# A four-layer graph network: row sums and powers of the first batch chunk by chunk, a corrected model time in the planner, and the last batch's gates with features on partitions

## The chip, the cores and the metric

The kernel runs on one core of one Trainium2 chip. The time is the device time of one execution in microseconds (us). All executions quoted are of the fast state: on one core the state is judged by the time alone, and none was set aside. Each profile is one execution; its span is 1.8 to 2.4 us shorter than the time of the same execution. "Product" below means a matrix product on TensorE.

## The reference, cut

32 graphs of 512 nodes with 128 features go through four layers. Each layer normalizes x per node, takes the positive part h, and adds the layer's output to x. A is `adj`, 512 x 512 per graph.

```python
def reference(x, adj, ...):
    h = relu(layernorm(x)); x = x + L0(h, adj)   # (D^-1/2 (A+I) D^-1/2) h W + b, leaky relu; D = row sums of A+I
    h = relu(layernorm(x)); x = x + L1(h, adj)   # elu of three projections, A and A^T times two of them, tanh
    h = relu(layernorm(x)); x = x + L2(h, adj)   # four sub-layers f1..f4 with A scaled by its row and column norms
    h = relu(layernorm(x)); x = x + L3(h, adj)   # m = tanh(A (h Wm)); r, z, n gates of a GRU; (1-z) n + z h
    return x
```

## The kernel before: the parts that the argument touches

The kernel doesn't issue its instructions as written. It records every operation with a model time, and a list scheduler (`Plan.order`) lays all 32 batches out in that model: a free engine takes, of its ready operations, the one whose due time is earliest. The result is a fixed order on each engine. In these kernels each engine follows that order and waits by semaphores. So a model time costs nothing by itself, but decides what stands in front of what.

```python
class Plan:
    def order(self):
        ...
            due = o.batch * PERIOD if o.batch < B - 1 else (B - 2) * PERIOD + ENDING
            o.key = (due - o.tail + o.later if o.rank is None else o.rank - 1e6, i)
        ...                         # event by event: an idle engine takes the ready operation of least key

    def t_act(n, pointers=0):                  # model time of a ScalarE operation of n columns
        return 0.09 + 0.093 * pointers + n / 1150
    def t_pow(n):                              # model time of a GpSimd power, n wide
        return 0.9 + 0.1 * n
```

The normalization in front of each layer (moments on VectorE, the power -1/2 on GpSimd, `nb` on VectorE, four `h` on ScalarE), the 512 x 128 transposition through DRAM, and `f`:

```python
        def normed(xin, out_tag, extra=None):
            ...                                                  # bn_stats and bn_aggr of 4 chunks -> mv
            # in moments(): v = variance + eps
            op("DVE", 0.08, lambda: nc.vector.tensor_scalar_add(v8.ap()[:, 0:NC], mv.ap()[:, :, 1], LN_EPS), ...)
            op("POOL", t_pow(n), lambda: nc.gpsimd.tensor_tensor(inv..., v8..., neg_half[:, :n], op=ALU.pow), ...)   # sc
            op("DVE", 0.08, ..., [mv, inv], [nb])
            for c in range(NC):
                op("ACT", t_act(D, 2), ..., [xin, nb, inv], [(h, {c})])          # h = relu(x * inv + nb)
        def turned(m, name):
            op("DVE", t_tt(N), lambda: nc.vector.transpose(blk..., m...), [m], [blk])
            for k in range(NC):
                op("SP", 0.4, lambda k=k: away(k), [blk], [(bounce, {k})], kb=64)      # turn_<name>, to DRAM
            op("SP", 0.4, lambda: nc.sync.dma_start(mT.ap(), bounce.tile), [bounce], [mT], kb=256)   # and back
        ...
        # row and column norms of A: to DRAM, spread over all partitions, put in order by ScalarE
        op("SP", 0.4, spread, [bounce], [spaced], kb=512)
        op("ACT", t_act(2 * N), lambda: nc.scalar.copy(rows..., spaced.ap().rearrange("p n k -> p k n")), [spaced], [rows])
        ...
            op("ACT", t_act(N, 1), ..., [ps, CF], [f_new])                             # f1 .. f4 = tanh(ps + b)
        ...
            f4 = turned(f[0], "f4r")                                                   # f4 back to rows
            tt(x3, lambda: nc.vector.tensor_add(x3, x2, turned_cols(f4)), ...)         # xr <- xr,f4r
        h3, _ = normed(x3, "h")
```

Where TensorE's plan has a gap of over 0.7 us, mostly in the first 60 us, filler products (`ps_idle`) are inserted to keep its clock up.

Names used below: `agg` is layer 0's aggregate and `lin` its product with W; `rep` is a projection of layer 1 after elu, `u` that layer's update; `sd` is a product with layer 2's weights plus its bias, which the aggregations with A take.

Of the kernel before, what the change touches and what calls it, by code (L numbers as in the profile page):

```python
# [13 lines left out]
F32 = mybir.dt.float32  # L14
AF = mybir.ActivationFunctionType
ALU = mybir.AluOpType
AX = mybir.AxisListType

P = 128
B, N, D = 32, 512, 128  # L20
NC = N // P
# [3 lines left out]
PERIOD = 30.0  # L25
ENDING = 6.0
SMALL = 16


SEVEN = {"last": 0 * 5 * D, "mid": 1 * 5 * D, "gates": 2 * 5 * D}  # L30
# [9 lines left out]
W_L2 = []  # L40
# [18 lines left out]



C_L1_NODE, C_L2 = 0, 1
C_COLS = C_L2 + 4 * len(L2_CHUNKS)



# [193 lines left out]
def gnn_stack(  # L260
# [21 lines left out]
    rf_sb = const.tile([P, len(L2_CHUNKS) * 2 * D], F32, name="rf_sb")  # L282
    cf_sb = const.tile([P, len(L2_CHUNKS)], F32, name="cf_sb")
    t_sb = const.tile([P, T_COLS], F32, name="t_sb")
    ident = const.tile([P, P], F32, name="ident")
    neg_half = const.tile([P, 2 * NC], F32, name="neg_half")

    def wt(col, n=D):
        return w_sb[:, col:col + n]
# [8 lines left out]
    def t_tt(n, pointers=0):  # L298
        return 0.065 + 0.058 * pointers + n / 960

    def t_ts(n):
        return 0.07 + n / 1920

    def t_act(n, pointers=0):
        return 0.09 + 0.093 * pointers + n / 1150

    def t_pool(n):
        return 0.15 + n / 450

    def t_pow(n):  # L310
        return 0.9 + 0.1 * n

    def op(*args, **kwargs):
        return plan.op(*args, **kwargs)

    def const_buf(name, ap):
        b = Buf(plan, name, name, None)
        b.tile, b.slot = ap, 0
        return b

    W1, W2F, W3, CS, RS, RF, CF, TS, ID, NH = (const_buf(n, t) for n, t in (
        ("w1", w_sb), ("w2", w_sb), ("w3", w_sb), ("c_sb", c_sb), ("r_sb", r_sb), ("rf_sb", rf_sb),
        ("cf_sb", cf_sb), ("t_sb", t_sb), ("ident", ident), ("neg_half", neg_half)))

    def mm(ps, out_of, lhs, rhs, n, start, stop, reads, later=0.0):
        op("PE", t_mm(n), lambda: nc.tensor.matmul(out_of(ps.ap()), lhs(), rhs(), start=start, stop=stop),  # L326
           reads, [ps], later=later)
# [9 lines left out]
    def setup():  # L337
# [1 line left out]

        op("POOL", 1.0, lambda: make_identity(nc, ident), [], [ID])  # L340
        op("POOL", 0.2, lambda: nc.gpsimd.memset(neg_half, -0.5), [], [NH])
        first = W_L2[0][0]

        def spread(lo, hi, to=None):
            return lambda: nc.sync.dma_start(
                r_sb[:, lo:hi] if to is None else to.ap()[:, :hi - lo], bass.AP(tensor=brow.tensor, offset=brow.offset + lo, ap=[[0, P], [1, hi - lo]]))
# [2 lines left out]
        op("AQ", 0.5, lambda: nc.scalar.dma_start(w_sb[:, :D], w[:, :D]), [], [(W1, {0})], kb=64)  # L349
        op("AQ", 0.5, lambda: nc.scalar.dma_start(  # L350
            r_sb[:, :D], bass.AP(tensor=brow.tensor, offset=brow.offset, ap=[[0, P], [1, D]])), [], [(RS, {0})], kb=64)
        op("SP", 0.5, lambda: nc.sync.dma_start(c_sb, bcol), [], [CS], kb=9, rank=2)
        op("SP", 0.5, lambda: nc.sync.dma_start(w_sb[:, D:first], w[:, D:first]), [], [(W1, {1})], kb=(first - D) / 2, rank=5)
        op("SP", 0.5, spread(D, R_L3_MSG), [], [(RS, {1})], kb=(R_L3_MSG - D) / 2, rank=5)
        op("SP", 0.5, spread(R_L3_MSG, R_COLS), [], [(RS, {2})], kb=(R_COLS - R_L3_MSG) / 2)
        hrz = plan.buf("s2", (P, N), "hrz")
        op("SP", 0.5, spread(R_L3_HRZ, R_L3_HRZ + 2 * D, hrz), [], [hrz], kb=D)
        op("DVE", 0.4, lambda: nc.vector.tensor_add(r_sb[:, R_L3_G:R_L3_G + 2 * D], r_sb[:, R_L3_G:R_L3_G + 2 * D], hrz.ap()[:, :2 * D]),
           [(RS, {2}), hrz], [(RS, {2})])
        raws = []  # L360
        for i in (0, 2, 3):
            lo, hi = RAW_L2[i][0], RAW_L2[i + 1][0] if i == 2 else RAW_COLS if i == 3 else RAW_L2[2][0]
            buf = plan.buf("s8", (P, NC, N), f"raw{i}")
            op("SP", 0.5, lambda buf=buf, lo=lo, hi=hi: nc.sync.dma_start(
                buf.ap().rearrange("p c n -> p (c n)")[:, :hi - lo], raw[:, lo:hi]), [], [buf], kb=(hi - lo) / 2, rank=3 if i == 0 else 6)
            raws += [(buf, lo)] * (2 if i == 0 else 1)
        op("SP", 0.5, lambda: nc.sync.dma_start(w_sb[:, W_L3_MSG:], w[:, first:]), [], [W3], kb=(W_COLS - W_L3_MSG) / 2)

        def block(i, col):
            buf, lo = raws[i]  # L370
# [48 lines left out]
    def program(b):  # L419
        plan.batch = b  # L420

        def buf(tag, shape=(P, N), name=None):
            return plan.buf(tag, shape, name)
# [3 lines left out]

        rows_shape = (P, NC, D)


        xt, a, aT = buf("s2", rows_shape, "x"), buf("s8", (P, NC, N), "a"), buf("s8", (P, NC, N), "aT")

        pieces = NC if b == 0 else 2

        def load(dst, src, kb, rank):

            n = NC // pieces
            for k in range(pieces):
                s = slice(k * n, (k + 1) * n)
                op("SP", 0.4, lambda s=s: nc.sync.dma_start(dst.ap()[:, s, :], src[:, s, :]),  # L440
                   [], [(dst, set(range(NC)[s]))], kb=kb / pieces, rank=None if b else rank)

        op("SP", 0.4, lambda: nc.sync.dma_start(xt.ap(), x[b]), [], [xt], kb=256, rank=None if b else 0)
        load(a, adj[b], 1024, 1)
        load(aT, adjt[b], 1024, 4)

        def moments(xin, v8):
            st, mv = buf("bn", (P, NC, nc.vector.BN_STATS_DIM)), buf("mv", (P, NC, nc.vector.BN_AGGR_DIM))
            for c in range(NC):
                op("DVE", 0.193, lambda c=c: nc.vector.bn_stats(st.ap()[:, c, :], xin.ap()[:, c, :]), [xin], [(st, {c})])  # L450
            for c in range(NC):
                op("DVE", 0.066, lambda c=c: nc.vector.bn_aggr(mv.ap()[:, c, :], st.ap()[:, c, :]), [(st, {c})], [(mv, {c})])
            op("DVE", 0.08, lambda: nc.vector.tensor_scalar_add(v8.ap()[:, 0:NC], mv.ap()[:, :, 1], LN_EPS), [mv], [(v8, {0})])  # L453
            return mv

        def normed(xin, out_tag, extra=None):


            v8 = buf("v8", (P, 2 * NC))
            n = NC  # L460
            mv = moments(xin, v8)
            if extra:
                extra(v8)
                n = 2 * NC
            inv = buf("sc", (P, 3 * NC))
            op("POOL", t_pow(n), lambda: nc.gpsimd.tensor_tensor(inv.ap()[:, :n], v8.ap()[:, :n], neg_half[:, :n], op=ALU.pow),  # L466
               [v8, NH], [(inv, {0})])
            at = 0
            if extra:
                at = 2 * NC  # L470
                op("DVE", 0.08, lambda: nc.vector.tensor_mul(inv.ap()[:, at:at + NC], inv.ap()[:, 0:NC], inv.ap()[:, NC:2 * NC]),
                   [(inv, {0})], [(inv, {1})])
            nb = buf("nb", (P, NC))
            op("DVE", 0.08, lambda: nc.vector.scalar_tensor_tensor(nb.ap(), mv.ap()[:, :, 0], -1.0, inv.ap()[:, at:at + NC],  # L474
                                                                   op0=ALU.mult, op1=ALU.mult), [mv, inv], [nb])
            h = buf("s2", rows_shape, out_tag)
            for c in range(NC):
                op("ACT", t_act(D, 2), lambda c=c: nc.scalar.activation(  # L478
                    h.ap()[:, c, :], xin.ap()[:, c, :], AF.Relu, bias=nb.ap()[:, c:c + 1],
                    scale=inv.ap()[:, at + c:at + c + 1]), [xin, nb, inv], [(h, {c})])  # L480
            return h, inv
# [157 lines left out]
                    sq.ap(), a.ap()[:, c, :], AF.Copy, accum_out=stat.ap()[:, c:c + 1]), [(a, {c})], [sq, (stat, {c})])  # L639
            op("DVE", 0.08, lambda: nc.vector.tensor_scalar_add(v8.ap()[:, NC:], stat.ap(), 1.0), [stat], [(v8, {1})])  # L640

        hr, inv0 = normed(xt, "h", degree)

        diag = buf("s2", rows_shape, "diag")

        def own(k, n):
            t = aT.ap()
            blocks = bass.AP(tensor=t.tensor, offset=t.offset + k * (N + P), ap=[list(t.ap[0]), [N + P, n], [1, P]])
            nc.gpsimd.tensor_tensor(diag.ap()[:, k:k + n, :], blocks, ident[:, None, :].to_broadcast([P, n, P]), op=ALU.add)

        n = NC if b else 1
        for k in range(0, NC, n):
            op("POOL", t_pool(n * P), lambda k=k, n=n: own(k, n), [(aT, set(range(k, k + n))), ID], [(diag, set(range(k, k + n)))])
        psh = plan.bank("agg")
        for c in range(NC):
            for lo, hi in ((0, c * P), (c * P, (c + 1) * P), ((c + 1) * P, N)):
# [71 lines left out]
        def spread():  # L728
            d = bounce.tile
            nc.sync.dma_start(spaced.ap().rearrange("p n k -> p (n k)"),  # L730
                              bass.AP(tensor=d.tensor, offset=d.offset, ap=[[0, P], [1, 2 * N]]))
# [50 lines left out]
        else:  # L782
# [10 lines left out]
        msg = buf("s2", rows_shape, "msg")  # L793
        tt(msg, lambda: nc.vector.tensor_add(msg.ap(), psm.ap().rearrange("p (c v) -> p c v", c=NC), along(r_sb, R_L3_MSG, D, NC)),
           N, [psm, (RS, {2})])
        psa = plan.bank("agg")
        aT2 = buf("s8", (P, NC, N), "aT2")
        load(aT2, adjt[b], 1024, None)
        aggregate(psa, msg, 0, aT2)
        mT = buf("s2", name="mT")  # L800
        op("ACT", t_act(N), lambda: nc.scalar.activation(mT.ap(), psa.ap(), AF.Tanh), [psa], [mT])

        g = buf("s8", (P, NC, 4 * D), "g")
# [110 lines left out]
```

## Time and profile before

| | before |
|---|---|
| median of 5 runs beside the changed kernel | 2319.75 us (2319.23 to 2321.92) |
| TensorE busy 1000 to 1500 us | 500.00 of 500 us |
| first layer-2 product (`ps_sd<-w_sb,f`) | 57.69 us |
| start of the last aggregation to the end of the span | 2301.6 to 2319.2: 17.6 us |
| TensorE's waits on `f` in the whole run | 3.8 us in 5 waits |

The 57.69 us is of an execution whose head cooled: after a wait of 2.10 us the granted clock was 0.50 from 38 to 40 us and 0.68 in the next 2 us. In the profiles of experiments 4, 6, 7 and 10, in which TensorE's order in the head is the same, the clock stayed at 1.00 there and the same product came at 55.1 to 55.7 us. So a difference of 2 us in this mark between two profiles can be one cold stretch, and the prediction took its base from a cold one.

The prediction below shows the busy table, stretches and waits. One more piece of the kernel before is needed as the yardstick: one pass of the chain that ends in f2, the second `f` of a batch's layer 2. It is the timeline from 1202 to 1210 us. Columns: start, duration (us), engine, line, operation, output<-inputs, sizes, count, and in brackets the idle time of the engine just before with what ended it.

```profile
1202.43 2.07 ACT L735 COPY rows<-spaced 128x1024 f32<-128x1024 f32 x1 [5.91 <-DMA spaced<-bounce]
1203.07 0.69 DVE L784 TENSOR_TENSOR xr<-xr,f4r 128x512 f32<-128x512 f32 x1 [0.21 <-DMA f4r<-turn_f4r]
...
1205.72 0.16 DVE L453 TENSOR_SCALAR v<-mv 128x4 f32<-128x4 f32 x1
...
1205.96 1.11 POOL L466 TENSOR_TENSOR sc<-v,neg_half 128x4 f32<-128x4 f32 x1 [2.57 <-DVE v L453]
1206.12 0.70 DVE L487 STREAM_TRANSPOSE blk<-h 128x512 f32<-128x512 f32 x1
...
1207.10 0.16 DVE L474 SCALAR_TENSOR_TENSOR nb<-mv,sc 128x4 f32<-128x4 f32 x1 [0.28 <-POOL sc L466]
1207.30 1.65 ACT L478 ACTIVATE h<-xr,nb,sc 128x128 f32<-128x128 f32 x4 [1.25 <-DVE nb L474]
1208.85 0.67 ACT L768 ACTIVATE f<-ps_agg,cf_sb 128x512 f32<-128x512 f32 x1
...
1209.77 0.59 PE L326 MATMUL ps_agg<-f,w_sb 128*128 128x512 f32 x1
```

Three batches meet here. `f4r`, `v`, `sc`, `nb` and `h` are layer 3 of batch b-1; `f` and the product are f2 of batch b; `rows` and `blk` are of batch b+1, whose layer-1 `h` is being transposed. On ScalarE f2 stands behind four `h`, so f2 hangs on `xr`, and `xr` on the transfer of `f4r`. The `v` stands **ahead** of `blk`. From the start of the `xr` add to the product it takes 6.7 us, and the product doesn't wait: there is no bracket on it.

### The profile page before, as it was taken

What the parts mean: (1) busy time and instruction counts of PE and PEld (TensorE: products, weight loads), DVE (VectorE), ACT (ScalarE), POOL (GpSimd) and SP (SyncE); (2) the same over time, 40 slices, a digit from 0 to 9 for tenths busy, and PEclk for the clock granted to TensorE, in tenths of its full rate; (3) what the DMA queues carried; (4) which work ended last, traced back from release to release, by engine and by line L of the source; (5) the groups of instructions that cost most, each with busy time, mean ns of one, the idle gap of its engine ahead of it and who ended that gap; (6) DMA issues with size and microseconds to landing.
All of it is one profiled execution on the core that took longest, in us unless ns stands there. A gap on an engine that the chain in (4) does not pass through costs nothing.

```text
span 2319.2 us, 28279 instructions
## 1 busy us (share of the span) xinstructions
PE 2301.0 (99%) x9682; PEld 1446.3 (62%) x9682; DVE 1530.8 (66%) x4132; ACT 946.4 (41%) x2018; POOL 262.6 (11%) x218
## 2 busy tenths in 40 slices
PE   9999999999999999999999999999999999999998
PEld 7656666666666566666666666666666666656665
DVE  5655666666667676676766676766766666767655
ACT  7323344334443344443344433444433444334412
POOL 3001101011111011010111101110101111101101
PEclk9999999999999999999999999999999999999999
DMA  7102332233222232222332322322223322223200
GB/s 261 46 10 64 105 94 75 81 101 107 76 91 82 82 109 81 87 79 86 105 100 83 91 82 82 109 81 88 78 86 105 107 76 91 82 82 105 77 6 27
DMA packets 133054, 200.82 MB, mean 87 GB/s; under 512 B 18992, under 2 KB 79920, under 8 KB 132912
## 3 DMA queue, kind: packets, MB, share of 16 engines
q1 hardware_dynamic: 132624, 198.90, 28.0%
q8 instruction: 76, 1.25, 0.2%
q14 instruction: 66, 0.54, 0.1%
q10 hardware_dynamic: 288, 0.13, 0.0%
HBM read 160.05 MB, written 38.93 MB: 86 GB/s over the span
## 4 chain that ended last, share of the span: by engine, by line
PE 91%; DMA 3%; DVE 3%; ACT 2%; POOL 1%; SPq 0%; issue 0%; DVEq 0%; ACTq 0%; POOLq 0%
PE ps_agg L326 61%; PE ps_seven L597 11%; PE ps_sd L326 9%; PE ps_upd L326 4%; PE ps_gate L326 2%; PE ps_msg L326 1%; DMA f4r<-turn_f4r 1%; PE ps_node L326 1%; PE ps_lin L326 1%; ACT h L478 1%; DMA turn_f4r<-blk 1%; POOL sc L466 1%; SPq L496 0%; ACT f L768 0%; DVE bn L450 0%
## 5 line engine op out<-in xcount | busy, mean ns | idle before, releaser
L326 PE MATMUL ps_agg<-aT,sd 128*128 128x512 f32 x1024 | 510.5, 594 | 0.1
L326 PE MATMUL ps_agg<-a,sd 128*128 128x512 f32 x1024 | 482.4, 592 | 0.0
L466 POOL TENSOR_TENSOR sc<-v,neg_half 128x4 f32<-128x4 f32 (+1 forms) x128 | 157.8, 1233 | 1638.6 <-DVE v L453 1361.8
L326 PEld LDWEIGHTS ps_agg<-a,sd 128*128 128x128 f32 x1024 | 184.6, 190 | 182.8 <-issue 178.4
L326 PE MATMUL ps_agg<-f,w_sb 128*128 128x512 f32 x448 | 229.6, 594 | 3.9 <-ACT f L768 3.8
L326 PEld LDWEIGHTS ps_agg<-aT,sd 128*128 128x128 f32 x1024 | 177.7, 191 | 83.0 <-issue 66.7
L326 PE MATMUL ps_sd<-w_sb,f 128*128 128x256 f32 x768 | 217.4, 380 | 0.5 <-ACT f L768 0.4
L478 ACT ACTIVATE h<-xr,nb,sc 128x128 f32<-128x128 f32 x384 | 158.2, 482 | 136.4 <-DVE nb L474 136.3
L597 PEld LDWEIGHTS ps_seven<-t_sb,s 128*128 128x128 f32 x1128 | 161.6, 191 | 78.1 <-issue 69.3
L326 PEld LDWEIGHTS ps_sd<-w_sb,f 128*128 128x128 f32 x768 | 136.6, 191 | 95.2 <-issue 76.5
L597 PE MATMUL ps_seven<-t_sb,s 128*128 128x128 f32 x1128 | 168.1, 275 | 0.0
L735 ACT COPY rows<-spaced 128x1024 f32<-128x1024 f32 x32 | 66.1, 2064 | 164.9 <-DMA spaced<-bounce 164.9
L326 PE MATMUL ps_agg<-aT,rep 128*128 128x512 f32 x256 | 131.3, 596 | 2.1 <-DVE rep L693 2.1
L326 PE MATMUL ps_agg<-a,rep 128*128 128x512 f32 x256 | 131.3, 596 | 0.0
L768 ACT ACTIVATE f<-ps_agg,cf_sb 128x512 f32<-128x512 f32 x128 | 87.2, 682 | 98.8 <-PE ps_agg L326 98.8
L326 PE MATMUL ps_agg<-aT,msg 128*128 128x512 f32 x256 | 124.9, 592 | 0.0
L487 DVE STREAM_TRANSPOSE blk<-f 128x512 f32<-128x512 f32 x29 | 20.6, 711 | 144.2 <-ACT f L768 144.2
L326 PE MATMUL ps_agg<-aT,h 128*128 128x256 f32 (+2 forms) x384 | 99.3, 381 | 0.2 <-ACT h L478 0.2
L597 PEld LDWEIGHTS ps_seven<-w_sb,f 128*128 128x128 f32 x512 | 75.9, 191 | 35.4 <-issue 27.7
L739 DVE TENSOR_TENSOR aT<-aT,rows 128x512 f32<-128x512 f32 x128 | 87.9, 687 | 14.7 <-PE ps_agg L326 14.6
L553 DVE TENSOR_TENSOR sd<-ps_sd,rf_sb 128x512 f32<-128x512 f32 x128 | 86.9, 679 | 15.5 <-PE ps_sd L326 15.4
L739 DVE TENSOR_TENSOR a<-a,rows 128x512 f32<-128x512 f32 x128 | 88.1, 689 | 13.6 <-PE ps_agg L326 13.5
(144 smaller groups left out, 3817.3 us busy)
## 6 DMA issues: line engine op xcount, KB each, us to landing
aT<-in_adjt SPq DMA_DIRECT2D x124, 512.0 KB, 5.2
a<-in_adj SPq DMA_DIRECT2D x62, 512.0 KB, 5.2
turn_turned<-blk SPq DMA_DIRECT2D x348, 64.0 KB, 1.8
turned<-turn_turned SPq DMA_DIRECT2D x87, 256.0 KB, 2.6
spaced<-bounce SPq DMA_DIRECT2D x32, 512.0 KB, 4.0
x<-in_x SPq DMA_DIRECT2D x32, 256.0 KB, 2.8
out<-xo SPq DMA_DIRECT2D x30, 256.0 KB, 2.0
turn_f4r<-blk SPq DMA_DIRECT2D x116, 64.0 KB, 1.8
```

Source lines behind the costliest of these rows:

```text
L326: op("PE", t_mm(n), lambda: nc.tensor.matmul(out_of(ps.ap()), lhs(), rhs(), start=start, stop=stop), reads, [ps], later=later)
L466: op("POOL", t_pow(n), lambda: nc.gpsimd.tensor_tensor(inv.ap()[:, :n], v8.ap()[:, :n], neg_half[:, :n], op=ALU.pow), [v8, NH], [(inv, {0})])
L478: op("ACT", t_act(D, 2), lambda c=c: nc.scalar.activation(h.ap()[:, c, :], xin.ap()[:, c, :], AF.Relu, bias=nb.ap()[:, c:c + 1], scale=inv ...
L487: op("DVE", t_tt(N), lambda: nc.vector.transpose(blk.ap().rearrange("p b (c r) -> p c b r", c=NC), m.ap().rearrange("p c (b s) -> p c b s" ...
L553: op("DVE", t_tt(N), lambda ps=ps, h=h: nc.vector.tensor_add(sd.ap()[:, 2 * h:2 * h + 2, :], ps.ap().rearrange("p (j v) -> p j v", j=2), s ...
L597: op("PE", t_mm(D), lambda j=j: nc.tensor.matmul(ps.ap()[:, k * H + j * D:k * H + (j + 1) * D], lhs()[:, j * P:(j + 1) * P], rhs(), start= ...
L735: op("ACT", t_act(2 * N), lambda: nc.scalar.copy(rows.ap().rearrange("p s (c n) -> p (s c) n", c=NC), spaced.ap().rearrange("p n k -> p k ...
L739: op("DVE", t_tt(N), lambda m=m, c=c, s=s: nc.vector.tensor_mul(m.ap()[:, c, :], m.ap()[:, c, :], rows.ap()[:, s, :]), [(m, {c}), rows], [ ...
L768: op("ACT", t_act(N, 1), lambda ps=ps, i=i, f_new=f_new: nc.scalar.activation(f_new.ap(), ps.ap(), AF.Tanh, bias=cf_sb[:, i:i + 1]), [ps, ...
```

## The change

Four things are changed. (1) The first batch's row sums (now on VectorE), powers (on GpSimd) and `h` are made chunk by chunk, and its `diag` moves to VectorE, so that the first aggregate starts earlier. (2) The head's transfers are ranked in a list. (3) The planner's model time of a GpSimd power is brought near to what the chip takes, 0.98 us for four wide instead of 1.3. (4) The last batch's layer 3 runs with features on partitions and in two halves of the nodes: biases ride on ScalarE, half the sigmoid's arithmetic goes away, and identity products turn the result back.

```diff
+FIRST = ["x0", "a0", "c", "raw0", "aT0", "w1", "r1", "raw2", "raw3"]
 ...
     def t_pow(n):
-        return 0.9 + 0.1 * n
+        return 0.35 + 0.157 * n
 ...                                        (six bias columns more in c_sb, cg_sb holds them scaled)
+        def normed_by_chunk(xin, out_tag):
+            mv = moments(xin, v8)
+            op("POOL", t_pow(NC), ...)                              # of the variances, four wide
+            for c in range(NC):
+                op("DVE", t_tt(N), lambda c=c: nc.vector.tensor_reduce(stat..., a.ap()[:, c, :], AX.X, ALU.add), ...)
+                op("DVE", 0.08, ...)                                # + 1
+                op("POOL", t_pow(1), ...)                           # ** -1/2, one wide
+                op("DVE", 0.08, ...); op("DVE", 0.08, ...)          # product of the two, nb
+                op("ACT", t_act(D, 2), ...)                         # h of the chunk
 ...
-        hr, inv0 = normed(xt, "h", degree)
+        hr, inv0 = normed_by_chunk(xt, "h") if b < 1 else normed(xt, "h", degree)
 ...
+        own_engine, own_name = (nc.vector, "DVE") if b < OWN else (nc.gpsimd, "POOL")     # diag
 ...
+        if b == B - 1:
+            gates_turned(x3, h3T, msg, aT2, mT)
+            return
 ...
+        def gates_turned(x3, h3T, msg, aT2, mT):
+            ...            # hn = (Whn h + b) / 2; per half: m = tanh(agg), gates in 128 x 256 banks
+            ...            # r', z' = tanh(x / 2 + b / 2); n = tanh((r'+1) hn + gi_n + b)
+            ...            # q = (z'+1) h, nw = (z'-1) n; xo = x3 + q^T / 2 - nw^T / 2 (products with +-I/2)
```

## The prediction

> **What bounds the kernel now.** I read the busy table first, then TensorE's busy time by stretch, its waits, and the timelines of the first 60 us and the last 30 us.
>
> ```profile
> PE 2301.0 (99%) x9682; PEld 1446.3 (62%) x9682; DVE 1530.8 (66%) x4132; ACT 946.4 (41%) x2018; POOL 262.6 (11%) x218
> ```
>
> ```profile
> 0.00:5.00 5.00, 3.60 (x17) 3.60 (x18) 1.23 (x9) 1.28 (x1) 0.74 (x7) 1.00 0.60 168
> ...
> 35.00:40.00 5.00, 3.54 (x6) 1.64 (x7) 4.54 (x8) 5.00 (x15) 0.40 (x1) 0.79 1.03 401
> 40.00:45.00 5.00, 5.00 (x11) 2.08 (x10) 4.00 (x12) 1.98 (x7) 1.27 (x1) 0.87 0.97 360
> ...
> 1000.00:1500.00 500.00, 500.00 (x2097) 313.14 (x2097) 340.23 (x914) 207.03 (x436) 54.49 (x42) 1.00 0.30 91
> ...
> 2310.00:2320.00 10.00, 1.74 (x11) 1.41 (x10) 5.92 (x18) 3.53 (x14) 3.94 (x8) 0.73 0.09 26
> ```
>
> In the second block (stretch, its length, then busy us with counts of PE, weight load, DVE, ACT, POOL; granted clock, DMA share, GB/s) the middle of the run has no free TensorE time: 500.00 of 500. So only three things can move the time: what TensorE must do, its gaps in the head, and what follows its last products. The same view for the filler products alone finds 9.48 us in 0 to 20 us and 4.87 in 20 to 40, so much of the head's "busy" is filler that keeps the clock up.
>
> ```profile
> PE ps_agg L326 <- ACT f L768: 3.8, 5, 1.1
> PE ps_agg L326 <- DVE rep L693: 2.1, 1, 2.1
> ```
>
> ```profile
> 31.14 2.06 ACT L735 COPY rows<-spaced 128x1024 f32<-128x1024 f32 x1 [0.89 <-DMA spaced<-bounce]
> 33.10 0.50 ACT L478 ACTIVATE h<-x,nb,sc 128x128 f32<-128x128 f32 x1
> 33.50 0.62 ACT L690 ACTIVATE rep<-sd 128x512 f32<-128x512 f32 x1
> ```
>
> Steady waits are only about 4 us (first line). The worst head wait is the second: `rep` of batch 0 stands behind `rows` (2.06 us) on ACT although its input was ready at 32.4.
>
> ```profile
> 2313.53 0.54 DVE L849 SCALAR_TENSOR_TENSOR u<-g 128x128 f32<-128x128 f32 x1
> 2313.99 0.54 DVE L857 TENSOR_TENSOR xo<-q,n 128x128 f32<-128x128 f32 x1
> ...
> 2315.72 0.48 DVE L857 TENSOR_TENSOR xo<-q,n 128x128 f32<-128x128 f32 x2
> ```
>
> At the end TensorE stops at 2311.7 and VectorE works alone until 2316.2; the output transfer ends the span at 2319.2.
>
> **What the Trainium skill says.** (1) "TensorE: Matmul & The Clock Gate", Part 1: the array runs at half clock after an idle window of about 3.4 us that runs freely, until it has been busy for one. The trace agrees in kind: after the 2.1 us wait the granted clock was 0.79 and 0.87 in two stretches of 5 us, that is 5 x (0.21 + 0.13) = 1.7 us lost. (2) The same page, engine queue depths: ScalarE and VectorE are strict first-in, first-out. The trace agrees: `rep` behind `rows`. (3) "SBUF — State Buffer", "Who interferes with whom": GpSimd and VectorE share a port pair, whoever has it blocks the other for the whole instruction. The trace agrees: a 128x4 `nb` op took 1.23 us beside a GpSimd `diag` op of 1.27, and 0.15 elsewhere.
>
> **The change, part by part.** I compared each engine's instruction order in both built programs.
>
> *Work.* Useful columns streamed by TensorE: 1,345,668 before, 1,346,692 after. The 1,024 new ones are the last batch's eight 128-column turns back (identity times one half): 8 x 0.22 = 1.8 us. Filler products drop from 60 to 44.
>
> *Ranks.* The first ten transfers stand in the same order as before, so the ranking itself gives nothing; `c_sb` only grows from 17 to 23 columns.
>
> *First chain by chunk.* Before: the last chunk of `a` is summed by 9.95, then an eight-wide power (1.65 us), two small VectorE ops, each 0.4 long beside GpSimd's `diag`, `h` from 13.03, first product 13.66, the aggregate's end 17.39. After: VectorE sums (0.6 each), a one-wide power (1.0 us for four-wide, so some 0.5 for one, an estimate), `diag` on VectorE (0.28): `h` from about 10.2 to 12.0. Now the transfer of `aT` bounds: first chunk at 11.63 in the trace, the last at 13.6. First product about 12.0, end 12.0 + 4 x 0.86 = 15.4. The six fold matmuls which ran before the aggregate now stand between it and `lin` (6 x 0.22 = 1.3), so `lin` starts at 16.8 against 18.50: **1.7 us**.
> Then `x1` no longer stands behind a stats op that waited 0.54 us for batch 1's input. `diag` of batch 1 will still meet `nb`. I get `h` of layer 1 at 24.3 against 26.59: **2.3**. In the new ACT order both `rep` stand ahead of `rows`, so layer 1's aggregation starts at 31.9 against 36.46: **4.6**, and seven fillers stand before it, so the 1.7 us of half clock should go.
> But some comes back. `rows` now comes after `zn`, at 33.4 to 35.4; behind it stand four `h` and four row sums before `agg_in` (39.8), so TensorE waits about 1.5 us there. VectorE has eight 0.6 us scalings and some twenty small ops between `rows` and `u`, so `u` starts at about 45.0 against 49.09. From `u` to the first layer-2 product takes 57.69 - 49.09 = 8.6 us, with enough filler work. That product moves from 57.69 to 53.6: head gain **4.1 us**, less about 0.5 for the risk of rival 1: **3.6**.
>
> *Steady state.* Same work; the order shifts a little. Two chains could newly bind. The third `f` of a layer now stands behind `y` and four `h` on ACT: in a traced batch the last update product ends at 1303.4 and `h` ends at 1310.0, 6.5 later; plus 0.6 for the `msg` op now in that chain and 0.7 for `f`: 7.9, against 8.0 us of TensorE work (4 x 0.86 + 0.89 + 0.86 + 2.57 + 0.22) before the product that needs it. It just fits. The `rep` chain has 0.5 us to spare. The old `f` waits have one more small product in front of them. Sum: **0.5 us** better.
>
> *Tail.* Before, from the start of the last aggregation (2301.5) to the end: 17.7 us. After: batch 30's message products stand before the last layer-2 product, which removes about 0.9 us of filler but may wait 0.5 for a transfer. More of the work is left for after that start (10.35 us against 9.87, of which 1.76 is new), so the start moves to about +0.5. From there: four half products 1.7, `hn` 0.9, the second half between gate products; the last gate product at 8.65; tanh 0.45, tanh of `n` 0.45, two VectorE steps of 0.4, eight turns interleaved, four adds of 0.28: the last `xo` at about 11.5, and 3.0 us for the transfer as before: 14.5. Gain 17.7 - 14.5 - 0.5 = **2.7 us**: eight bias adds of 0.68 us and the chunk-by-chunk blend leave VectorE, biases ride on ACT for nothing.
>
> Sum: 3.6 + 0.5 + 2.7 = 6.8. 2320.0 - 6.8 = **2313**.
>
> **Rivals.** (1) *The clock falls early.* The fillers end at about 10.2 and the first product comes at 12.0. The traced gap of 0.94 us did no harm, that of 2.1 did. If 1.8 us does, the first aggregate ends up to 1.6 later: about 2314.5. For it: nothing useful stands there now; against: one gap under half the window. (2) *A steady wait per batch.* If the `f` or `rep` chain misses by 0.3 us in 28 batches, that is 8 us, all gain gone: 2321. For it: slack of 0.1 us, VectorE at 66%; against: the chain's ops are back to back in the trace, with nothing between. (3) *Head gain given back.* If VectorE's backlog or the head transfers (DMA share about 1.0 up to 45 us) hold the first layer-2 product where it was, 3 us of gain go: 2316. (4) *Better than this.* If all four `f` waits vanish and `u` isn't held: 2307.
>
> **Range and chances.** Head 3.6 ± 1.5, tail 2.7 ± 1, steady from 3 better to 6 worse: 2313, from **2307 to 2319** in 8 of 10. 2% is 46 us; nothing here is of that size. Within 2%: 0.985; faster by more: 0.005; slower by more: 0.01.
>
> **What would show it.** First aggregate product at about 12.0 and its end at 15.4 (17 if rival 1); layer 1's aggregation at about 32 at full clock; a TensorE wait of about 1.5 us on `agg_in`; first layer-2 product at 53.6; steady waits on `f` under 4 us in all; last TensorE product within 2.5 us of the last VectorE op, and some 14.5 us from the last aggregation's start to the end. The prediction is wrong if a wait repeats in every batch, or if the work done by 60 us is the same as before.

## The result, and the profile after

| | before | after |
|---|---|---|
| median of 5 runs | 2319.75 us (2319.23 to 2321.92) | 2343.13 us (2341.07 to 2346.90) |
| ratio of the fast runs | | 1.0102, 95% interval 1.0088 to 1.0117 |
| TensorE busy 1000 to 1500 us | 500.00 | 491.70 |
| first layer-2 product | 57.69 us | 57.56 us |
| last aggregation to the end | 17.6 us | 2330.1 to 2344.2: 14.1 us |

Here and below a ratio is the mean time of one kernel's fast runs over the mean of the other's fast runs of the same rounds, so it is not quite the ratio of the medians. The time was predicted at 2313.0, at most 2319; it is 23 us longer than before. That is inside 2%, and plainly outside the predicted range.

The busy line of the page, TensorE's waits in the whole run (waited for: us in total, times, longest), and a stretch from the middle of the run (columns as in the prediction):

```profile
PE 2306.4 (98%) x9664; PEld 1447.6 (62%) x9664; DVE 1539.7 (66%) x4146; ACT 939.1 (40%) x2002; POOL 252.9 (11%) x210
```

```profile
PE ps_agg L335 <- ACT f L869: 18.1, 24, 2.0
PE ps_agg L335 <- DVE sd L653: 5.3, 11, 0.7
PE ps_agg L335 <- DVE diag L749: 3.4, 1, 3.4
PE ps_lin L335 <- ACT agg L764: 1.5, 1, 1.5
```

```profile
1000.00:1500.00 500.00, 491.70 (x2055) 307.47 (x2054) 334.91 (x888) 201.47 (x430) 52.47 (x42) 1.00 0.30 89
```

Waits on `f` went from 3.8 us in 5 to 18.1 in 24; waits on `sd`, which before had none, are 5.3 us. The wait on f2 returns with nearly every batch, some 71.5 us apart, from 350 us on. The list of waits counts only idle time after a product's modelled end. An estimate from start to start (each distance between two products less the lower quartile of the same pair of tiles and shapes in all fourteen profiles, 300 to 2230 us) closes the account: products that take `f` start 25.3 us late in all, before 5.8; aggregations of `sd` 8.7, before 1.8; the whole is 36.5, before 7.7. Less the 3.5 us of the shorter tail, that is about the 25.0 us between the two spans. The same chain as shown of before, in the timeline of the changed kernel from 850 to 859 us:

```profile
850.34 2.06 ACT L836 COPY rows<-spaced 128x1024 f32<-128x1024 f32 x1 [5.94 <-DMA spaced<-bounce]
850.99 0.69 DVE L885 TENSOR_TENSOR xr<-xr,f4r 128x512 f32<-128x512 f32 x1 [0.26 <-DMA f4r<-turn_f4r]
...
852.31 1.65 ACT L578 ACTIVATE h<-xr,nb,sc 128x128 f32<-128x128 f32 x4
...
853.99 0.71 DVE L587 STREAM_TRANSPOSE blk<-h 128x512 f32<-128x512 f32 x1 [0.26 <-ACT h L578]
854.62 0.13 DVE L527 TENSOR_SCALAR v<-mv 128x4 f32<-128x4 f32 x1
...
854.90 1.05 POOL L566 TENSOR_TENSOR sc<-v,neg_half 128x4 f32<-128x4 f32 x1 [3.63 <-DVE v L527]
855.98 0.17 DVE L574 SCALAR_TENSOR_TENSOR nb<-mv,sc 128x4 f32<-128x4 f32 x1 [0.90 <-POOL sc L566]
856.18 1.65 ACT L578 ACTIVATE h<-xr,nb,sc 128x128 f32<-128x128 f32 x4 [2.22 <-DVE nb L574]
...
857.73 0.67 ACT L869 ACTIVATE f<-ps_agg,cf_sb 128x512 f32<-128x512 f32 x1
...
858.45 1.12 PE L335 MATMUL ps_agg<-f,w_sb 128*128 128x512 f32 x2 [0.42 <-ACT f L869]
```

Now `blk` stands **ahead** of `v`. It waits 0.26 us for the `h` of batch b+1, which stood behind `rows`, and runs 0.71; only then comes `v`, whose input had been ready. From the start of `xr` to the product it is 7.46 us, and TensorE waits 0.42. In the five batches of the kernel before where the product does wait, the same distance is 6.51: the chain itself has become 0.95 us longer. In 7 of the 24 waits of the changed kernel it is 7.10, because `f4r` landed so late that `blk` no longer waited for its `h`; these seven, with 7.3 of the 18.1 us, are a longer chain and a late `f4r` together.

The head, in stretches of 2 us of TensorE alone (stretch, length, busy with count, granted clock, DMA share, GB/s):

```profile
8.00:10.00 2.00, 0.82 (x8) 1.00 1.01 406
10.00:12.00 2.00, 0.00 (x0) 0.77 1.05 407
12.00:14.00 2.00, 1.77 (x4) 0.50 1.04 398
14.00:16.00 2.00, 2.00 (x8) 0.50 1.05 420
16.00:18.00 2.00, 2.00 (x7) 0.52 1.01 408
```

The fillers end at 8.83, the first useful product waits 3.4 us for `diag` and comes at 12.23, and the whole first aggregate runs at half clock. Granted clocks of 0.77, 0.50, 0.50 and 0.52 in four stretches of 2 us are 3.4 us lost.

The tail, from the timeline: the first of the last aggregation's products and the last VectorE operation.

```profile
2330.10 1.25 PE L335 MATMUL ps_agg<-aT,msg 128*128 128x256 f32 x5
```

```profile
2340.98 0.51 DVE L498 TENSOR_TENSOR xo<-xr,ps_gate 128x128 f32<-128x128 f32 x2 [0.39 <-PE ps_gate L335]
```

### The profile page after: what moved, and what is told of

Read it like the earlier page. It is cut to its first block, busy times and chain, and to the rows that moved or that the text cites. A ratio compares the mean times of both kernels' runs of the same rounds, so it can differ in the third digit from the quotient of the medians.

```text
span 2344.2 us, 28196 instructions
## 1 busy us (share of the span) xinstructions
PE 2306.4 (98%) x9664; PEld 1447.6 (62%) x9664; DVE 1539.7 (66%) x4146; ACT 939.1 (40%) x2002; POOL 252.9 (11%) x210
## 4 chain that ended last, share of the span: by engine, by line
PE 74%; DMA 7%; DVE 7%; ACT 6%; SPq 2%; POOL 2%; issue 1%; POOLq 0%; DVEq 0%; ACTq 0%
PE ps_agg L335 51%; PE ps_seven L697 8%; PE ps_sd L335 7%; PE ps_upd L335 4%; DMA spaced<-bounce 3%; ACT h L578 3%; PE ps_gate L335 2%; SPq L596 2%; DVE blk L587 2%; ACT rows L836 2%; POOL sc L566 1%; ACT f L869 1%; DMA f4r<-turn_f4r 1%; PE ps_msg L335 1%; PE ps_node L335 1%
## 5 line engine op out<-in xcount | busy, mean ns | idle before, releaser
L566 POOL TENSOR_TENSOR sc<-v,neg_half 128x4 f32<-128x4 f32 (+1 forms) x127 | 151.2, 1191 | 1665.2 <-DVE v L527 1308.2
L335 PE MATMUL ps_agg<-f,w_sb 128*128 128x512 f32 x448 | 231.4, 599 | 18.3 <-ACT f L869 18.1
L335 PEld LDWEIGHTS ps_agg<-aT,sd 128*128 128x128 f32 x1024 | 172.5, 191 | 77.3 <-issue 44.7
L335 PE MATMUL ps_agg<-aT,rep 128*128 128x512 f32 x256 | 126.6, 593 | 1.2 <-DVE rep L794 1.1
L738 ACT ACTIVATE sq<-a 128x512 f32<-128x512 f32 x124 | 77.6, 626 | 123.2 <-DMA a<-in_adj 121.5
L335 PE MATMUL ps_agg<-a,rep 128*128 128x512 f32 x256 | 126.2, 592 | 0.0
L335 PE MATMUL ps_agg<-aT,msg 128*128 128x512 f32 (+1 forms) x264 | 121.0, 579 | 0.0
L335 PEld LDWEIGHTS ps_agg<-f,w_sb 128*128 128x128 f32 x448 | 75.6, 191 | 43.0 <-ACT f L869 23.3
L587 DVE STREAM_TRANSPOSE blk<-h 128x512 f32<-128x512 f32 x87 | 61.8, 710 | 61.0 <-ACT h L578 60.8
```

The source lines that it names most:

```text
L335: op("PE", t_mm(n), lambda: nc.tensor.matmul(out_of(ps.ap()), lhs(), rhs(), start=start, stop=stop), reads, [ps], later=later)
L566: op("POOL", t_pow(n), lambda: nc.gpsimd.tensor_tensor(inv.ap()[:, :n], v8.ap()[:, :n], neg_half[:, :n], op=ALU.pow), [v8, NH], [(inv, {0})])
L587: op("DVE", t_tt(N), lambda: nc.vector.transpose(blk.ap().rearrange("p b (c r) -> p c b r", c=NC), m.ap().rearrange("p c (b s) -> p c b s" ...
L738: op("ACT", 0.73, lambda c=c: nc.scalar.activation(sq.ap(), a.ap()[:, c, :], AF.Copy, accum_out=stat.ap()[:, c:c + 1]), [(a, {c})], [sq, ( ...
```

## The experiments

Twelve kernels were run, each in five rounds or more (4 to 21 timed runs each), all correct. "1.0018 (1.0006 to 1.0031)" is the ratio to the kernel before with its 95% interval; the kernel before had medians of 2318.97, 2319.4, 2320.97 and 2319.25 us in the four groups (1 to 4, 5 to 8, 9 to 11, 12). The groups ran on different chips, so kernels of different groups are better compared by their ratios than by their medians; the half width of an interval is 1.5 to 3 us. Where the expectations speak of "the third f", they count along ScalarE's order (f4 of the batch before, f1, f2): it is f2. The diffs are shortened.

### 1 to 4: which part of the change

**1.** The changed kernel, old model time.

```diff
     def t_pow(n):
-        return 0.35 + 0.157 * n
+        return 0.9 + 0.1 * n
```

> The changed kernel with one line put back: the planner's model time of a GpSimd power is 0.9 + 0.1n again instead of 0.35 + 0.157n. No instruction of it changes, only the order in which the planner lays instructions on the engines. Theory A (the shorter model time took slack out of the order in the middle batches, so that f and sd come late there): the steady waits on f and sd fall from about 24 us to under 6, the tail keeps its 14 us, the head its first layer-2 product at about 57.5, so 2343 - 20 - a few of slowed products: 2317 to 2319, faster than the kernel before by about 2. Theory B (the new head shifts the phase of the whole plan, and that causes the waits): they stay, about 2343. Theory C (the turned gates of the last batch change priorities in the steady part): also about 2343.

Measured: 2324.32 us, 1.0018 (1.0006 to 1.0031). Its waits on `f`: 8.6 us in 10; none on `sd`.

**2.** The kernel before, new model time alone (the same line the other way).

> The kernel before with that one line alone changed: 0.35 + 0.157n. Theory A: the order of the middle batches becomes that of the changed kernel (h ahead of the third f on ScalarE), with about 24 us of waits on f and sd between 100 and 2250 us; 2320 + 22 to 27 = 2342 to 2347. Theories B and C: nothing happens, 2318 to 2322, waits on f about 4 us as before.

Measured: 2341.86 us, 1.0095 (1.0082 to 1.0109). TensorE's waits:

```profile
PE ps_agg L326 <- ACT f L768: 12.6, 24, 1.7
PE ps_agg L326 <- DVE sd L553: 5.5, 11, 0.7
```

The time is at the edge of what theory A expected, with 18 us of recorded waits for 24. The order that the expectation names, `h` ahead of f2 on ScalarE, stands in the kernel before as well and isn't what changed; experiments 5 and 6 look at what did.

**3.** The head alone, with old model time and the last batch in rows.

```diff
-        if b == B - 1:
+        if b == B:                      # never
             gates_turned(x3, h3T, msg, aT2, mT)
```

> The kernel before with the head of the change alone (row sums and powers chunk by chunk, diag on VectorE, ranked transfers); the old model time, and the last batch's layer 3 in rows as before. Theory A with a head that gains nothing (the array cools in the wait for the transposed adjacency and gives back what the chunks win): first layer-2 product at 57 to 58, 2318 to 2321. Theory B: the waits on f of some 20 us come with the head, 2340 or more. If the head had its predicted gain: 2316.5.

Measured: 2325.86 us, 1.0026 (1.0014 to 1.0039). First layer-2 product at 54.73; waits on `f` 7.8 us in 10. Half clock in one stretch (0.53 and 0.61 from 12 to 16 us).

**4.** The turned gates alone, with old model time.

```diff
-        hr, inv0 = normed_by_chunk(xt, "h") if b < 1 else normed(xt, "h", degree)
+        hr, inv0 = normed(xt, "h", degree)
-OWN = 1
+OWN = 0
```

> The kernel before with the turned gates of the last batch alone; head and model time as before. From the start of the last aggregation to the end the changed kernel took 14.1 us against 17.7, and 1.3 us more work stands before: theory A expects 2320 - 2.3 = 2316.5 to 2318.5, with first layer-2 product still at 57.7 and steady waits under 6 us. Theory C: steady waits of 20 us come with it, 2340.

Measured: 2315.39 us, 0.9983 (0.9970 to 0.9997), 1 us below the expected range. Waits on `f` 3.9 us in 6. The first layer-2 product came at 55.31, not 57.7: the head didn't cool in this execution.

What follows. Taking the ratios times 2319.4: the model time costs 22.0 us, the head 6.0, and the turned gates gain 3.9. The sum is +24.1, and the whole change measured +23.7 (each with some 3 us of uncertainty). The model time is the cause of nearly all of it (theory A); neither a shift by the head nor the turned gates bring the waits of 24 batches (B and C fall). Two expectations were clearly missed. The head alone was to be worth nothing and loses 6 us, although its first layer-2 product is 3 us ahead of the cooled profile of the kernel before, and 0.3 us or more ahead of the old heads that stayed warm: it is overtaken later, by waits on `f` of 7.8 us for 3.8. And putting the constant back leaves 2324, not 2318, with 8.6 us of such waits.

### 5 to 7: what the order did

**5.** The changed kernel with its new model time, and one pair swapped after planning. A comparison of the built programs showed 26 swaps on VectorE and no difference on any other engine.

```diff
+def moved(done):                        # v of batch b - 2 ahead of blk of batch b
+    for o in [o for o in done if o.mark == "blk"]:
+        near = [n for n in done[done.index(o) + 1:] if n.engine == "DVE"][:3]
+        for n in near:
+            if n.mark == "v" and n.batch == o.batch - 2:
+                done.remove(n); done.insert(done.index(o), n)
-        plan.kept_warm(plan.order(), idle_products, 1.3)
+        plan.kept_warm(moved(plan.order()), idle_products, 1.3)
```

> The changed kernel with its new model time, and one pair of VectorE instructions swapped in 26 batches: v (the input of layer 3's power) ahead of blk (the transposition of the next batch's h). Nothing else moves on any engine. In the changed kernel the product that needs the third f comes 7.1 to 7.5 us after the add of f4r, in the kernel before 6.5: theory V says that this is v standing 0.95 us behind blk. Then the 6.5 comes back, waits of under 0.95 us vanish, those on f fall from 18.1 us to 3 to 8, and with slowed products the time falls by 12 to 19: 2324 to 2331, the waits on sd (5 us) staying. Rival R: the old order only moves the wait to the transfer of f4r, or the wait comes from other moved instructions: f waits stay above 12 us, 2336 to 2344.

Measured: 2324.43 us, 1.0022 (1.0012 to 1.0032). TensorE's waits (the helper shifts the line numbers):

```profile
PE ps_agg L349 <- DVE sd L669: 6.1, 14, 0.7
PE ps_agg L349 <- ACT f L885: 3.5, 5, 0.9
```

**6.** The kernel before with the reverse swap, again in 26 batches and nothing else (`blk` also passes the `s` that stands between the two, as it does in the changed kernel).

```diff
+            if n.mark == "blk" and n.batch == o.batch + 2:      # blk ahead of v
+                done.remove(n); done.insert(done.index(o), n)
```

> The kernel before (old model time, old head and tail) with the reverse swap: blk ahead of v in 26 batches, nothing else. Theory V: the chain from the add of f4r to the product that needs f goes from 6.5 to about 7.4 us, its slack of 0.3 to 0.6 us is used up, f waits go from 4 to 15 to 20 us, and the time to 2331 to 2341. Rival R: 2318 to 2323.

Measured: 2344.51 us, 1.0104 (1.0090 to 1.0118), a little more than expected. Part of it is the clock: two of its waits on f2, of 2.24 and 2.07 us, were each followed by half clock (0.50 from 574 to 576 and from 1008 to 1010 us), an estimated 1.7 us each. TensorE's waits:

```profile
PE ps_agg L340 <- ACT f L784: 22.2, 26, 2.2
```

What follows. The pair is shown both ways: swapped out of the changed kernel it gives back some 19 us (1.0102 to 1.0022), swapped into the kernel before it costs 24. One VectorE instruction of 0.13 us behind one of 0.71 is the mechanism of these; the model time of the power did it only by making the planner place them so. The waits on `sd` aren't touched by the swap: they belong to the rest of the new order, and were not taken apart. By the start-to-start estimate they are the larger rest: in experiment 5 products that take `f` start 6.1 us late, as before, and aggregations of `sd` 10.1, before 1.8.

**7.** With f2 ahead of the four `h` on ScalarE, in the kernel with the turned gates alone (27 batches).

```diff
+            if len(acts) == 4 and all(n.mark == "h" and n.batch == o.batch - 1 for n in acts):
+                done.remove(o); done.insert(done.index(acts[0]), o)       # o is the f behind them
```

> The kernel with the turned gates alone (2315.4 us), and in 27 batches the third f ahead of the four h on ScalarE, nothing else moved. The f no longer hangs on the power and on the transfer of f4r: its 3.9 us of waits should vanish, some 4 to 5 us with the slowed products: 2310 to 2312. Rival: h comes 0.7 us later, its transposition and the message products of layer 3 with it, and TensorE waits there instead: 2315 to 2320.

Measured: 2324.34 us, 1.0022 (1.0015 to 1.0030), 9 us worse than without, and outside both expectations. The waits on f2 are gone, and no other wait over 1.5 us is on the list; yet the batches are on average 71.0 us apart instead of 70.6 (from `xr` to `xr`). Start to start, products that take `f` gain 6.4 us over experiment 4, and products in the aggregations of `sd` and the products with `hT` among them lose some 16, mostly 0.05 to 0.3 us at a time. At the rival's place, the message products of layer 3, nothing is lost. VectorE's idle time before `blk` until ScalarE's `h` grew from 15.4 us in 15 waits to 34.7 in 33, and in one batch looked at (1139 us) `s` and `sd` of layer 2 stand behind that `blk`. So the later `h` probably costs through `blk` on VectorE again; this is read from the traces, and no experiment tested it.

### 8: the cold clock of the head

**8.** Experiment 1 with 13 more fillers before the first aggregate.

```diff
+                agg = o.batch == 0 and out and any(x.name == "ps_agg_0" for x in o.bufs) and not begun
-                if gap > self.SHORT:
-                    n = int(min(gap, cold) / self.COLD + max(gap - cold - 0.1, 0.0) / self.WARM)
+                if gap > self.SHORT or agg:
+                    n = int(...) + (13 if agg else 0)
```

> The changed kernel with the old model time (2324.3 us) and 13 more filler products (13 x 0.2225 = 2.9 us) in the gap of 3.1 us before the first aggregate, so that TensorE does not cool. If the cold clock is what the head loses: granted clock 1.00 from 12 to 18 us, the first aggregate over by about 15.6 instead of 18, the work of batch 2 some 2.5 us earlier than in that kernel, and 2321 to 2322.5 at the end. Rival: those 2.5 us are given back in later waits on f (its slack hangs on the transfer of f4r), and the end stays at 2324.

Measured: 2314.86 us, 0.9979 (0.9972 to 0.9985), 9.5 us better than experiment 1. Granted clock 1.00 from 10 to 60 us; the fillers overran a little, so that the aggregate starts at 12.67; first layer-2 product at 55.24 against 57.25 (56.34 in experiment 11, the same head with one cold stretch). So the head itself gained 2.0 us, near the expected 2.5, but the time is 6 us below the expected range. The other 7.5 came later, in part as fewer waits on f2 (3.6 us in 6 against 8.6 in 10), which nobody expected.

### 9 to 12: the transfer in front of the chain

In the queue, `spaced` (512 KB, batch b+1) was issued between the four `turn_f4r` (64 KB each) and `f4r` (256 KB). In these four kernels it is issued ahead of the `turn_f4r`, in 26 batches; nothing else moves on any engine.

```diff
+        near = [n for n in done[:done.index(o)] if n.engine == "SP"][-4:]      # o is spaced
+        if len(near) == 4 and all(n.mark == "f4r" and n.batch == o.batch - 2 for n in near):
+            done.remove(o); done.insert(done.index(near[0]), o)
```

**9.** In experiment 1 (the change with the old model time).

> The changed kernel with the old model time (2324.3 us, 8.6 us of waits on f in the profile), and in 26 batches the transfer of spaced (512 KB) issued ahead of the four turn_f4r instead of between them and f4r; nothing else moves. In that kernel f4r took 4.5 us to land in a batch with a wait, 3.3 in the kernel before, with spaced in flight at the same time. If the waits on f are f4r being slowed by spaced: f4r lands in under 3 us, waits on f fall from 8.6 to under 3 us and the time to 2315 to 2319. Rival: the turn_f4r are now slowed by spaced instead, f4r lands as late, and the time stays at 2322 to 2327.

Measured: 2311.92 us, 0.9960 (0.9948 to 0.9973), 12.4 us better than experiment 1 and 3 us below the expected range. No wait on f2 is left. The view of transfers (KB each, median us to landing), first of experiment 1, then of this kernel:

```profile
f4r<-turn_f4r SPq DMA_DIRECT2D x29, 256.0 KB, 3.3
```

```profile
f4r<-turn_f4r SPq DMA_DIRECT2D x29, 256.0 KB, 2.6
```

Its profile happens to answer the question of the head as well. Its head has the same instructions as experiment 1's, but in this execution the fillers ran slowly for longer and ended at 10.15 instead of 8.81:

```profile
8.00:10.00 2.00, 2.00 (x20) 1.00 0.99 398
10.00:12.00 2.00, 0.64 (x5) 1.00 1.07 412
12.00:14.00 2.00, 2.00 (x13) 1.00 1.06 407
14.00:16.00 2.00, 2.00 (x17) 1.00 1.03 420
```

The gap was 1.36 us, the clock stayed at 1.00, `lin` started at 16.19 and the first layer-2 product came at 53.31. In experiment 1 these were 19.52 and 57.25. So the cold first aggregate costs 3.3 us at `lin`. Of the 3.9 us at the layer-2 product, part is a second cold stretch in experiment 1: after a wait of 1.98 us on `agg` the clock was 0.51 and 0.64 from 52 to 56 us. The profiled execution is the fastest of experiment 9's five (2309.58 us), so other executions may have cooled.

**10.** In experiment 4 (the turned gates alone).

> The kernel with the turned gates alone (2315.4 us, 3.9 us of waits on f), with the same move of spaced. If f4r is slowed by spaced: waits on f under 1 us, 2310 to 2312. Rival (the turn_f4r are slowed instead): 2314 to 2318.

Measured: 2310.54 us, 0.9957 (0.9945 to 0.9970).

**11.** In experiment 8 (old model time, more fillers).

> The changed kernel with the old model time and the 13 more fillers (2314.9 us, 3.6 us of waits on f, work done up to 4.6 us earlier than in the kernel before by the middle of the run, of which 3.5 are lost again), with the same move of spaced. If f4r is slowed by spaced: the lead is kept, waits on f under 1 us, 2309 to 2312. Rival: 2313 to 2318.

Measured: 2311.18 us, 0.9955 (0.9942 to 0.9969).

**12.** In the changed kernel as it is, with the new model time.

> The changed kernel as it is, with the new model time, and in 26 batches the transfer of spaced issued ahead of the four turn_f4r; nothing else moves. Two causes may add up in its 18.1 us of waits on f: the chain from the add of f4r to the product that needs f is 7.5 us long against about 7.0 us which the old order has from that add to that product when f4r is early, and f4r itself is late in every third batch or so. If both: f4r is no longer late, but 0.3 to 0.5 us of wait stay in each of some 27 batches, 9 to 13 us on f in all, those on sd (5 us) stay, and the time is 2330 to 2338. If the late f4r is all: waits on f under 4 us and 2318 to 2325.

Measured: 2321.42 us, 1.0009 (1.0003 to 1.0016). TensorE's waits:

```profile
PE ps_agg L348 <- DVE sd L666: 6.0, 14, 0.7
...
PE ps_agg L348 <- ACT f L882: 0.3, 1, 0.3
```

This head has the order of the changed kernel's, and in this execution it stayed at clock 1.00: the gap was 1.60 us, `lin` came at 16.39 and the first layer-2 product at 54.19, for 19.91 and 57.56 in the changed kernel's cooled profile (experiment 5 cooled too: 57.35).

What follows. `f4r` is slowed by `spaced`, and with `spaced` out of the way the head's loss is gone: the change with the old model time is 9 us faster than the kernel before instead of 4 slower (by the ratios). Experiments 9 to 11 agree within 1.4 us, so that, once f2 doesn't wait, no gain of the new head is measured beside the turned gates; with intervals of 3 us either way, one of a few us isn't excluded.

In experiment 12 the sum of two causes that I expected was wrong, and the number of the other reading came true (2318 to 2325, waits on `f` under 4), but not quite for its reason. Earlier `spaced` also means earlier `rows`, so the `h` of batch b+1 is there when `blk` comes up: in the batch at 842 us `blk` starts with no wait, `v` follows at +3.33 us from the start of `xr` instead of +3.63, and the product at +7.23 instead of +7.46 has no wait. The order is still the bad one, and it still just fits. So the chain of the changed kernel reads in full: `spaced` late, `rows`, `h`, `blk`, and behind `blk` on VectorE `v`, the power, `nb`, `h`, f2, TensorE. What stays between experiment 12 and 9 is 9.5 us by the medians (12.5 between the profiles), of which some 6 are recorded as waits on `sd`; start to start, aggregations of `sd` are 10.6 us late in experiment 12 and 1.7 in 9.

Left open: why `f4r` lands later in some kernels whose steady order is the same on every engine (the kernel before and experiments 1, 3 and 4: 5, 10, 10 and 6 waits); I only showed that they all but vanish (one wait of 0.4 us in experiment 10, none in 9 and 11) when `spaced` doesn't lie across. How often a head cools is open too: of the three profiles with the changed kernel's head two cooled.

Experiments 9, 10 and 11 beat both kernels, by 9 to 10 us over the kernel before (by the ratios).

## Why the prediction was wrong, point by point

- **Steady state: the step that failed.** The prediction checked two chains that "could newly bind", f3's ("It just fits") and that of `rep`, and both held: no wait on either is in the steady part. The chain of f2, which already had the only steady waits of the kernel before, it dismissed with "The old `f` waits have one more small product in front of them", and booked "0.5 us better". The new order measured 22 us worse (experiment 2), some 19 of them through f2 (experiment 5). The extra product of 0.2 us was there; the swap of `blk` and `v` on VectorE, 0.95 us of chain, stood in the same comparison of orders and wasn't followed to what it feeds. The aggregations of `sd`, which start some 7 us later than before, the prediction didn't consider at all; what delays them stays open.
- **Rival 2** had the right kind, "a wait that repeats in every batch", and the wrong chain and size: 0.3 us in 28 batches (8 us) against 18.1 us in 24 waits on f2, and 5.3 us on `sd`. Its argument against, "the chain's ops are back to back in the trace, with nothing between", was read from the old trace; a new order is precisely what can put something between.
- **Head.** The chunked chain came as predicted: `h` from 10.1 to 12.0, for "about 10.2 to 12.0", and the first product at 12.23 for "about 12.0". Where the clock stayed up (experiment 9) the steps after it came out nearly to the number: `lin` 16.19 for 16.8, `u` 45.63 for 45.0, first layer-2 product 53.31 for 53.6. In the changed kernel it was 57.56, because rival 1 was true, and dearer than its "up to 1.6": the fillers ended 1.4 us earlier than I took them to, the whole aggregate ran at half clock, and the cost was about 3.4 us (57.56 against 54.19 in experiment 12). Its 1.8 us of gap was also called "under half the window", and half of 3.4 is 1.7. The gain was over-sized from the other side too: its base of 57.69 held a cold stretch of its own. Against the 55.1 of experiment 6, with the old head warm, the warm new head gains 1.8 (experiment 9), not 4.1. Layer 1's aggregation came at 35.80 for 31.9, at full clock as predicted. A wait of 1.5 us came, as large as predicted, but at 52.35 on `agg` of batch 1 for `lin`, not near 39.8 on `agg_in`: its size is luck.
- **Rival 3** foresaw the first layer-2 product held where it was. In the changed kernel it was (57.56 for 57.69), but by the cold clock, not by VectorE's backlog or the transfers. What the head gives back after that, in experiment 3, are waits on f2 for a late `f4r`, which the rival doesn't name.
- **Small slips in its working**, none of which decides anything: `lin` of the kernel before starts at 18.34, not 18.50; from 1303.4 to 1310.0 it is 6.6 us, not 6.5 (its 7.9 fits 6.6); the old tail is 17.6 us.
- **Tail.** Right: 14.1 us for 14.5, and 3.9 us gained for 2.7 (experiment 4, with an interval of 0.7 to 7.0).
- **Ranks.** Nothing in the runs speaks for an effect; they weren't run alone.
- **The skill's statements.** First-in, first-out on VectorE is the very mechanism: `v` behind `blk`. I used it for `rep` behind `rows` only. The clock's window runs freely, the page says, and these traces agree: waits of nearly the same length at the same place cooled the array in one execution and not in another. A wait of 1.98 us before `lin` was followed by clocks of 0.51 and 0.64 in experiment 1 and of 1.00 in experiment 8; one of 2.10 us before layer 1's aggregation by 0.50 in the kernel before, one of 2.04 at the same place by 1.00 in experiment 6. The prediction went by the length of the gap alone.

## What to carry to other kernels

In a kernel whose orders come from a planner, a model time is a scheduling decision: making one constant true, while others stay false (`rows` is modelled at 0.98 us and takes 2.06), can move an instruction to the wrong side of another. Where the orders of two builds differ, follow every swapped pair to what hangs on it, first of all on chains that already wait. And when a change moves the time, put back one line at a time: here one constant carried 22 of the 23.7 us, and one pair of instructions some 19. A mark read from one profile, such as the first layer-2 product here, can be off by a cold stretch of 1.7 us or more: look at the granted clock before it serves as a base.

## What the Trainium skill lacked or had wrong

- "TensorE: Matmul & The Clock Gate", "Why this matters for your kernels", advises to keep idle gaps under about 3 us. Here shorter gaps cooled the array: 2.67 us in experiment 3 (clock 0.53 and 0.61 in the two stretches of 2 us from 12 us on), 2.24 in experiment 6, 2.10 in the kernel before, and 1.83 in experiment 11 (0.59 and 0.56 in the two from 50 us on). One of 2.40 us did not (experiment 8), nor did those of 1.60 and 1.36 (experiments 12 and 9). Part 1 of the page does say that the window runs freely; the advice leaves out that a gap well under it can cool. What it cost in one place was 1.7 us, or 3.4 us where the gap was over 3 us (estimates from the granted clock).
- "SBUF — State Buffer", "Door 1: The DMA port swizzle", says that reads which leave a line of 16 bytes pay a penalty, without a figure for ScalarE. The copy `rows`, which reads every eighth float32, took 2.06 us for 1,024 columns; the copy `hT<-turned`, also from SBUF, which reads runs of 32 neighbours, took 0.61 for 512. That the stride is the reason wasn't tested.
- No page gives the time of a power on GpSimd: 1.05 to 1.11 us for 128x4 here, 1.64 for 128x8, 0.56 for 128x1 (medians).
- "DMA: Bandwidth & Descriptors", "Queues, rings and completion order", says that descriptors are taken in ring order on each engine. That agrees with `f4r` behind `spaced`, but the page has no figure for a transfer behind a larger one of the same queue: 3.3 us to landing for 256 KB, against 2.6 with `spaced` issued earlier.
